# Splitting a ring of four PSUM banks into two and two in an eight-stage model kernel

## The chip, the cores and the metric

The kernel runs on one core of a Trainium2 chip. The metric is the device time of one execution in microseconds (us), from the first to the last instruction with what the device adds around them. Lower is better.

The engines are named as in the profile: PE is TensorE (PEld its weight loads), DVE is VectorE, ACT is ScalarE, POOL is GpSimd, SP is SyncE, whose queue issues most transfers. PSUM, where PE writes, has eight banks of 2 KB per partition here; one bank is a tile of 128 x 512 float32.

## The reference, cut to what matters

Four layers, each of a sequence part and a feed-forward part with a residual and a norm after each, on four sequences of 1024 tokens with 128 features. Only the last three parts run while the change is at work: the feed-forward part of layer 2 (pairs of a token and one of its two experts), the recurrence of layer 3 and its experts.

```python
def _L3_attn_ref(resid, ...):
    x = resid * lax.rsqrt(jnp.mean(resid * resid, -1, keepdims=True) + EPS) * norm_w
    skip = x @ skip_w.T
    xe = x @ in_w.T
    ...
    xs = jax.nn.silu(xc.transpose(0, 2, 1))
    delta = jax.nn.softplus(xs @ wd1.T @ wd2.T + wd2_b)
    A = -jnp.exp(A_log)
    Bm = xs @ wb.T
    Cm = xs @ wc.T
    def step(h, inp):
        d_l, b_l, c_l, x_l = inp
        h = jnp.exp(d_l[:, :, None] * A) * h + (d_l * x_l)[:, :, None] * b_l[:, None, :]
        y_l = jnp.einsum('ben,bn->be', h, c_l)
        return (h, y_l)
    _, ys = lax.scan(step, h0, (...))
    y = ys.transpose(1, 0, 2) + xs * W_D
    y = (y * jax.nn.silu(skip)) @ out_w.T
    return resid + y

def _L3_ffn_ref(x, Wr, br, W1, b1, W2, b2):
    probs = jax.nn.softmax(x @ Wr + br, axis=-1)
    ...
    gate = probs * keep
    h = jax.nn.relu(jnp.einsum('bth,ehf->betf', x, W1) + b1[None, :, None, :])
    y = jnp.einsum('betf,efh->beth', h, W2) + b2[None, :, None, :]
    return jnp.einsum('bte,beth->bth', gate, y)
```

Left out are a convolution of four taps along the tokens, which gives `xc`, and the choice of the most probable of eight experts up to a sum of 0.8, which gives `keep`. The scan runs over the tokens, with 256 channels of 16 states. All eight experts are computed for every token, and weighted by `gate`, which is zero where an expert isn't kept.

## The kernel before

The first 1350 us or so (layers 0 to 2) have PSUM pools of their own, which the change leaves alone. Then `l3_pools` (L1676) opens the pools of the last stage. `banks(...)` (L88) makes one pool per tag with so many banks each, and `psb` (L113) opens a tile of one bank under a tag. Before the change eight banks go to four tags: `y0` and `y1` with one bank each for the sums over the states, `da` with two for the decay, and `ff` with four for everything else.

`l3` (L1595) walks over eight halves: four sequences, two halves of 512 tokens. For each half `l3_scan` (L1816) does 16 steps, one per state. A step loads two rows (`bn`, `cn`) through SP's queue, multiplies on POOL (`db`, L1846), takes an exponential on ACT (`da`, L1850, into a `da` bank), scans along the tokens on DVE (L1851), multiplies on POOL again (`hc`, L1862), and PE adds `hc` into the `y0` and `y1` banks (`pys`); from the second sequence on, every second `hc` is first added to the one before it by a transfer that POOL issues (L1867). `hc` has four buffers, so POOL waits when PE is late with `pys`.

Between these steps the program lays other work in small pieces, in this order: the end of the half before (`l3_sum`, `l3_finish`: output projection `po`, norm, router `prl`, gates `gt`), the preparation of the next half (`l3_prepare`: `pt`, `pxe`, `pdb`, then the two `pd` tiles, which stay open together from their matmul through a chain on ACT and DVE until `ud` and `dl` are written, L1810 and L1811), what is left of a dispatch, the pairs of layer 2 (`l2_ffn`: `pt`, a `ph` of 128-column pieces with the weights `wx`, a `py`; its `l2_combine` opens `py0` and a norm tile), and three or four pieces of the last experts. Two gates per half (`psk`, L1894) go into `ff` as well.

The last experts (`l3_experts`, L1639) take the finished halves in order, a block of eight experts per half. One expert (`l3_ffn`, L1959) is four `ph` tiles of 128 x 512, each turned into `hh` by a Relu on ACT (L1977), then one `py` tile of 16 products (32 matmul records), which DVE adds to `h_acc` in four pieces with the gate as factor (L1993). Before a block, `l3_ffn_head` opens `pgt` and `pb2`; after it comes the last norm (a `pmv` tile, L155) and the output. Weights come as 512 KB transfers on SP's queue (`wh`, three buffers). A block may begin once its half's gates are there and four steps old. When the last half's end is through and the block under way is finished, all these pools are closed and one pool of eight `ff` banks takes their place for the last block (L1656 to L1658).

What sets the order: each engine runs its own queue in order. The program is written as above, but the framework (`TileContext` with `schedule_with_timeline_sim=True`) makes the order of each engine when the kernel is compiled: of the instructions whose inputs and buffers it believes ready it issues the one that stands first in the program. An instruction that opens a tile is ready only when a buffer of its tag has been given back by the last reader. So the size of a pool decides how far the engines run ahead and in which order, and at run time the same order is kept with semaphores for the waits. In the part that is concerned no order is written out by hand.

Of the kernel before, what the change touches and what calls it, by code (L numbers as in the profile page):

```python
# [58 lines left out]
class Net:  # L59
# [1579 lines left out]
    def l3_experts(self, fp):  # L1639


        c3 = self.c3
        heads, self.wh = [], {}

        def others():

            while len(heads) < 2 and c3["todo"] and ("all" in c3 or c3["todo"][0]["age"] > 3):
                heads.append((c3["todo"].pop(0), []))
            return heads[1:]

        i = 0
        while True:
            others()
            if "all" in c3 and c3["banks"]:

                c3["banks"].close()  # L1656
                c3["banks"] = None
                c3["ctx"].enter_context(self.banks(ff=8))  # L1658
            if heads:
                u = heads[0]  # L1660
                if not u[1]:
                    yield from self.l3_ffn_head(*u, fp)
                yield from self.l3_ffn(*u, i, fp, others)
                heads.pop(0)
                i += NE
            elif "all" in c3:
                return
            else:
                yield
# [6 lines left out]
    def l3_pools(self, ctx):  # L1676
        tc = self.tc
        sp = ctx.enter_context(tc.tile_pool(name="ssm", bufs=1))
        wp = ctx.enter_context(tc.tile_pool(name="ssm2", bufs=2))
        banks = ctx.enter_context(self.banks(y0=1, y1=1, da=2, ff=4))  # L1680
        self.mtags = dict(t="ff", h=("ff",), o="ff")
        self.c3.update(sp=sp, wp=wp, ctx=ctx, banks=banks)

# [257 lines left out]
    def l3_ffn_head(self, u, head, wp):  # L1941

        nc, c3, h = self.nc, self.c3, u["h"]
        ff = lambda s, n: self.psb("ff", s, n)
        acc = wp.tile([P, 4, D], F32, name="h_acc")
        head.append(acc)
        pg = ff([NE, 4, P], "pgt")
        for c in range(4):
            self.tr(pg[:, c, :], u["gt"][:, c, :])
        gT = wp.tile([NE, 4, P], F32, name="gT", bufs=1)  # L1950
        nc.scalar.copy(gT, pg)
        yield
        pb = ff([P, 4, D], "pb2")
        for c in range(4):
            self.mm(pb[:, c, :], gT[:, c, :], c3["b2"])
        nc.vector.tensor_add(acc, pb, self.xN[u["b"]][:, 4 * h : 4 * h + 4, :])
        yield

    def l3_ffn(self, u, head, i0, wp, others):  # L1959

        nc, c3, b, h, gt, acc = self.nc, self.c3, u["b"], u["h"], u["gt"], head[0]
        ff = lambda s, n: self.psb("ff", s, n)
        NK = F3 // P
        x = self.xT[b][:, h * 512 : h * 512 + 512]
        ahead = None
        for e in range(NE):
            if i0 + e == 0:
                for k in range(2):
                    self.l3_weights(k, wp)
            self.l3_weights(i0 + e + 2, wp)  # L1970
            w = self.wh.pop(i0 + e)
            hs = []
            for k in range(NK):
                ph = ff([P, 512], "ph")
                self.mm(ph, w[:, k * P : (k + 1) * P], x)
                ht = wp.tile([P, 512], F32, name="hh", bufs=6)
                nc.scalar.activation(ht, ph, AF.Relu, bias=self.col("h_b1", i=e * NK + k))  # L1977
                hs.append(ht)
                yield
            py = ff([P, 4, D], "py")  # L1980
            for c in range(4):
                for k in range(NK):
                    self.mm(
                        py[:, c, :],
                        hs[k][:, c * P : (c + 1) * P],
                        w[:, F3 + k * D : F3 + (k + 1) * D],
                        k == 0,
                        k == NK - 1,
                    )
                if c == 1:  # L1990
                    yield
            for c in range(4):
                nc.vector.scalar_tensor_tensor(  # L1993
                    acc[:, c, :],
                    py[:, c, :],
                    gt[:, c, e : e + 1],
                    acc[:, c, :],
                    ALU.mult,
                    ALU.add,
                )  # L2000
            yield

            if e >= NE - 3:
                if ahead is None and others():
                    ahead = self.l3_ffn_head(*others()[0], wp)
                if ahead is not None:
                    next(ahead, None)
        for f in ahead or ():
            pass
        self.norm(wp, acc, b, 4 * h, 4, last=True, ps=ff, act=True)  # L2010

# [193 lines left out]
```

## Time and profile before

| what | us |
|---|---|
| median of 3 runs | 2294.14 (2287.42 to 2300.56) |
| the profiled execution | 2289.61 |
| its span, first to last instruction | 2287.8 |
| PE busy over the span | 1974.5 (86%) |
| POOL busy over the span | 1023.3 (45%) |
| first product of the first half on POOL (`db`, L1846) | 1386.3 |
| first tile of the last experts (`pgt`) | 1541.3 |
| last product of the last half on POOL (`hc`, L1862) | about 2150 |
| last matmul of the last experts | 2279.3 |

The profile is of one execution. Its page cuts the span into 40 slices of 57 us; the digit of an engine is its busy share in tenths, PEclk the clock that TensorE was granted, in tenths of full speed:

```profile
PE   6667979879999999999989876589888989898998
DVE  7457743424355565665555556686777787877521
ACT  6543443332244444444555456476767786767443
POOL 5100230000023235224243429988789979888500
PEclk9757989979999999999999987799999999999999
```

The change concerns the slices from the 25th on. In the views of groups a line holds the kernel's line, engine, operation, the tiles written and read, the shape, the count, then the busy time and the mean ns of one, and after the bar the idle time of the engine just before them and what ended it. A float32 product shows as two matmul records.

### The profile page before, as it was taken

To read this page: it belongs to the slowest core of one execution; us is meant where nothing else is said; L and a number is where in the kernel's file an instruction comes from. 1 tells how busy PE (TensorE), PEld (TensorE's weight loads), DVE (VectorE), ACT (ScalarE), POOL (GpSimd) and SP (SyncE) were. 2 spreads that over 40 slices of the span, in tenths; PEclk is the share of its full clock that TensorE was granted. 3 is DMA by queue.
4 is the path that set the end of the run, shared out by engine and by line. 5 is a ranking of instruction groups with operands and counts; after the bars stand their busy time and mean duration, and the time that the engine had idled before them with its cause. 6 is when DMAs were issued, how large, how long until landed. Compare 5 with 4: busy or idle time off the path is not lost.

```text
span 2287.8 us, 46393 instructions
## 1 busy us (share of the span) xinstructions
PE 1974.5 (86%) x17806; PEld 1382.2 (60%) x17806; DVE 1351.7 (59%) x3693; ACT 1207.2 (53%) x2621; POOL 1023.3 (45%) x812
## 2 busy tenths in 40 slices
PE   6667979879999999999989876589888989898998
PEld 3455655444477777787767664346555656565666
DVE  7457743424355565665555556686777787877521
ACT  6543443332244444444555456476767786767443
POOL 5100230000023235224243429988789979888500
PEclk9757989979999999999999987799999999999999
DMA  3000110005000010031223147456776666676421
GB/s 107 0 15 23 30 39 1 19 10 174 1 3 2 3 35 15 17 91 46 76 70 88 32 142 231 127 182 196 202 204 178 177 169 192 175 208 178 122 60 51
DMA packets 138558, 211.10 MB, mean 92 GB/s; under 512 B 18597, under 2 KB 75936, under 8 KB 137952
## 3 DMA queue, kind: packets, MB, share of 16 engines
q1 hardware_dynamic: 126192, 173.87, 24.7%
q0 software_dynamic: 12144, 34.26, 7.1%
q8 instruction: 140, 2.29, 0.4%
q14 instruction: 82, 0.67, 0.1%
HBM read 160.29 MB, written 23.16 MB: 80 GB/s over the span
## 4 chain that ended last, share of the span: by engine, by line
PE 40%; DVE 13%; ACT 11%; issue 4%; DMA 2%; POOL 1%; SPq 0%; ACTq 0%; DVEq 0%; POOLq 0%
PE py L127 7%; PE ph L127 6%; PE po L1126 5%; DVE db L1851 5%; PE pqk L127 4%; PE pa_m L127 4%; PE kp_mo L127 3%; PE pr L1196 2%; PE pv L127 2%; PE pys L127 2%; ACT hh L1977 2%; ACT da L1850 1%; PE pt L131 1%; PE kp_mo L131 1%; ACT xN L174 1%
## 5 line engine op out<-in xcount | busy, mean ns | idle before, releaser
L1059 POOL TENSOR_TENSOR qt<-r_q,sb_c_turn 128x256 f32<-128x256 f32 (+1 forms) x256 | 164.0, 661 | 448.5 <-ACT r_q L1051 442.9
L1862 POOL TENSOR_TENSOR hc<-db,cn 128x1024 f32<-128x1024 f32 x128 | 312.9, 2463 | 63.5 <-PE pys L127 27.1
L127 PEld LDWEIGHTS py<-wh,hh 128*128 128x128 f32 x2048 | 248.6, 193 | 85.6 <-issue 36.1
L1846 POOL TENSOR_TENSOR db<-ud,bn 128x1024 f32<-128x1024 f32 x112 | 284.1, 2593 | 12.7 <-DMA wh<-in_wH 6.2
L127 PE MATMUL py<-wh,hh 128*128 128x128 f32 x2048 | 257.1, 278 | 22.9 <-ACT hh L1977 12.5
L127 PE MATMUL ph<-xT,wh 128*128 128x512 f32 x512 | 250.3, 606 | 16.8 <-ACT hh L1977 5.9
L1977 ACT ACTIVATE hh<-ph,sb_cols 128x512 f32<-128x512 f32 x256 | 170.6, 681 | 131.9 <-PE ph L127 105.5
L1117 DVE TENSOR_TENSOR a<-pa_m,sb_c_near 128x256 f32<-128x256 f32 x256 | 96.7, 420 | 202.6 <-PE pa_m L127 202.6
L1074 ACT ACTIVATE kN<-kp_mo,sb_c_trig 128x128 f32<-128x128 f32 x448 | 130.2, 372 | 132.0 <-PE kp_mo L131 122.2
L1850 ACT ACTIVATE da<-dl,aneg 128x512 f32<-128x512 f32 x224 | 153.1, 689 | 77.8 <-DVE db L1851 76.6
L127 PE MATMUL pys<-hc,sb_c_ident 128*128 128x512 f32 x324 | 159.7, 621 | 29.3 <-POOL hc L1862 21.3
L1851 DVE TENSOR_TENSOR_SCAN db<-da,carry,db 128x512 f32<-128x512 f32 x128 | 158.0, 1268 | 21.1 <-POOL db L1846 11.9
L1851 DVE TENSOR_TENSOR_SCAN db<-da,db 128x512 f32<-128x512 f32 x128 | 149.6, 1207 | 9.5 <-POOL db L1846 6.0
L127 PEld LDWEIGHTS ph<-xT,wh 128*128 128x128 f32 x512 | 89.8, 194 | 98.1 <-issue 57.1
L1993 DVE SCALAR_TENSOR_TENSOR h_acc<-py,gt,h_acc 128x128 f32<-128x128 f32 x256 | 71.8, 343 | 124.6 <-PE py L127 124.0
L127 PE MATMUL pqk<-xT,wE 128*128 128x256 f32 x512 | 136.8, 390 | 8.2 <-ACT coT L1193 4.2
L127 PEld LDWEIGHTS pys<-hc,sb_c_ident 128*128 128x128 f32 x324 | 61.0, 199 | 96.7 <-issue 60.6
L729 POOL DMA_INDIRECT orows<-o,ix x20 | 18.9, 944 | 186.6 <-DVE o L727 160.4
L127 PEld LDWEIGHTS pqk<-xT,wE 128*128 128x128 f32 x512 | 89.0, 194 | 22.0 <-DVE cv L1036 8.1
L131 PE MATMUL pt<-sb_c_ident,xN 128*128 128x128 f32 x224 | 54.4, 343 | 51.4 <-ACT xN L174 32.2
L1193 ACT COPY coT<-pt 128x512 f32<-128x512 f32 x64 | 37.6, 587 | 116.1 <-PE pt L131 116.1
L127 PE MATMUL po<-ht,wD 128*128 128x512 f32 x192 | 94.3, 598 | 0.0
(456 smaller groups left out, 4340.2 us busy)
## 6 DMA issues: line engine op xcount, KB each, us to landing
wx<-in_wF SPq DMA_DIRECT2D x92, 384.0 KB, 3.3
bn<-rows SPq DMA_DIRECT2D x128, 256.0 KB, 5.0
cn<-rows SPq DMA_DIRECT2D x128, 256.0 KB, 4.3
wh<-in_wH SPq DMA_DIRECT2D x64, 512.0 KB, 4.1
hc<-hc POOLq DMA_DIRECT2D x47, 512.0 KB, 6.6
xrows<-zero SPq DMA_DIRECT2D x4, 1472.0 KB, 11.9
xg<-xrows SPq DMA_DIRECT2D x20, 256.0 KB, 3.0
yrows<-ys SPq DMA_DIRECT2D x20, 256.0 KB, 3.3
```

Of the source, the lines that this page charges most:

```text
L127: return self.nc.tensor.matmul(out=out, lhsT=lhsT, rhs=rhs, start=start, stop=stop)
L131: self.nc.tensor.transpose(out, in_, self.ident[0:n, 0:n])
L1059: nc.gpsimd.tensor_mul(u["qt"][:, m, a:], u["q"][:, a:], c2["turn"][:, m, o + a : o + 2 * P])
L1074: self.nc.scalar.activation(u["kN"][:, c, m, :], pk[:, c, :], AF.Copy, scale=trig[:, k, m : m + 1])
L1117: nc.vector.tensor_mul(u["a"][:, i, :, :], pa[i], self.c2["near"][:, None, :].to_broadcast([P, 2, P]),)
L1126: self.nc.tensor.matmul(out=u["po"][self.HALF[j], i, c, :], lhsT=lhsT, rhs=rhs, start=key not in u["begun"], stop=True, skip_group_check=True,
L1846: nc.gpsimd.tensor_mul(db, ud, bc[0])
L1850: nc.scalar.activation(da, dl[:, ec, :], AF.Exp, scale=aneg[:, j : j + 1])
L1851: nc.vector.tensor_tensor_scan(db[:, ec, :], da, db[:, ec, :], carry[:, ec, n : n + 1] if h else 0.0, ALU.mult, ALU.add,)
L1862: nc.gpsimd.tensor_mul(hc, db, bc[1])
L1977: nc.scalar.activation(ht, ph, AF.Relu, bias=self.col("h_b1", i=e * NK + k))
L1993: nc.vector.scalar_tensor_tensor(acc[:, c, :], py[:, c, :], gt[:, c, e : e + 1], acc[:, c, :], ALU.mult, ALU.add,)
```

## The change

The four banks `ff` of the last stage become two tags of two banks each: `ff` and `ex`. The last experts' tiles (`pgt`, `pb2`, `ph`, `py`) now open under `ex`; the preparation, the ends of the halves, the router, the gates, the norms (the last one too) and the pairs of layer 2 stay under `ff`. For the last block, the one pool of eight becomes `ff` with two and `ex` with six. No instruction is added or removed, and no tile changes its size.

```diff
@@ l3_experts @@
                 c3["banks"].close()
                 c3["banks"] = None
-                c3["ctx"].enter_context(self.banks(ff=8))
+                c3["ctx"].enter_context(self.banks(ff=2, ex=6))
@@ l3_pools @@
-        banks = ctx.enter_context(self.banks(y0=1, y1=1, da=2, ff=4))
+        banks = ctx.enter_context(self.banks(y0=1, y1=1, da=2, ff=2, ex=2))
         self.mtags = dict(t="ff", h=("ff",), o="ff")
@@ l3_ffn_head @@
-        ff = lambda s, n: self.psb("ff", s, n)
+        ff = lambda s, n: self.psb("ex", s, n)
@@ l3_ffn @@
-        ff = lambda s, n: self.psb("ff", s, n)
+        ff = lambda s, n: self.psb("ex", s, n)
...
-        self.norm(wp, acc, b, 4 * h, 4, last=True, ps=ff, act=True)
+        self.norm(wp, acc, b, 4 * h, 4, last=True, ps=self.bank("ff"), act=True)
```

## The prediction, made before the change was run

> **What bounds the kernel now.** I read the page's row of slices first, then the busy time by stretches, then the groups on TensorE, and last the timeline of the experts alone. The change touches only what runs after about 1372 us, when the recurrence has its own PSUM pools.
>
> Busy time of each engine by stretch. The columns are the stretch, its length, busy us of PE, PEld, DVE, ACT and POOL with instruction counts, the granted clock, the DMA share and GB/s:
>
> ```profile
> 1372.00:1456.00 84.00, 54.46 (x200) 33.36 (x199) 54.02 (x93) 51.12 (x112) 78.12 (x47) 0.78 0.64 201
> 1456.00:1541.00 85.00, 61.00 (x247) 37.24 (x248) 70.36 (x114) 50.65 (x100) 79.45 (x35) 0.88 0.51 157
> 1541.00:1650.00 109.00, 97.69 (x513) 66.64 (x511) 74.59 (x154) 75.66 (x163) 87.72 (x50) 0.97 0.67 199
> 1750.00:1850.00 100.00, 90.48 (x430) 56.39 (x429) 77.42 (x163) 81.83 (x155) 91.08 (x49) 1.00 0.65 176
> 2050.00:2150.00 100.00, 93.21 (x464) 60.90 (x463) 72.34 (x137) 66.94 (x103) 85.82 (x43) 1.00 0.67 182
> 2150.00:2221.00 71.00, 65.14 (x368) 46.60 (x366) 22.60 (x78) 31.88 (x52) 0.00 (x0) 1.00 0.22 65
> 2221.00:2288.00 67.00, 58.18 (x320) 41.54 (x320) 10.79 (x42) 24.64 (x41) 0.00 (x0) 0.93 0.16 48
> ```
>
> Three stages. Until 1541 POOL is the bound (158 of 169 us busy) and PE has slack (115 of 169). From 1541, where the last experts begin, to 2150 PE and POOL are both near 90%. After 2150 only experts are left and PE runs nearly alone. PE's work is fixed, and experts left over at 2150 run in the end stage, so from 1541 on the end is PE's work plus PE's idle time. In 1541 to 2150 PE is busy 550 of 609 us. These 59 us are what the change can shrink or stretch. Their causes stand in the groups on PE from 1541 to 2150 (busy, mean ns, then idle time before them and who ended it):
>
> ```profile
> L127 PE MATMUL py<-wh,hh 128*128 128x128 f32 x1536 | 194.4, 278 | 21.7 <-ACT hh L1977 11.8 <-ACT ys L1510 5.1 <-ACT db L1785 2.2
> L127 PE MATMUL ph<-xT,wh 128*128 128x512 f32 x391 | 192.5, 605 | 13.2 <-ACT hh L1977 5.9 <-ACT ys L1510 3.4 <-DVE h_acc L1993 2.2
> L127 PE MATMUL pys<-hc,sb_c_ident 128*128 128x512 f32 x204 | 98.5, 605 | 7.8 <-DMA hc<-hc 7.8
> L127 PE MATMUL ph<-xgT,wx 128*128 128x128 f32 x153 | 21.4, 282 | 4.9 <-ACT ys L1510 1.5 <-ACT dl L1811 1.4 <-ACT ln_sd L164 1.1
> L127 PE MATMUL psk<-xnT,sb_s_in 128*128 128x512 f32 x24 | 12.6, 608 | 3.7 <-ACT hh L1977 3.7
> ```
>
> Experts (`wh`) wait for ACT to release pairs' and preparation's banks (`ys`, `db`), and a gate (`psk`) waits for an expert's bank. This is how a full shared ring looks.
>
> **How many banks each side needs.** For every PSUM tile I took the time from its first matmul to the end of its last reader, pairing matmuls and readers in order. From 1541 to 2150 the experts hold 0, 1, 2, 3, 4 banks for 46, 274, 215, 69 and 6 us (1.5 on average); the others hold 1.2. All four are held for 156 of 609 us. Mean holds: expert `ph` 2.8 us, expert `py` 7.5, pair `ph` 5.0, pair `py` 2.2, `pd` 16.2 (two at once), `prl` 12.1, `pxe` 10.2. From 1372 to 1541, without experts, the others hold three banks for 44 us and four for 43 us.
>
> **Part by part.** No instruction is added, removed or resized, and no DMA; only which tile may open when. The order on each engine is made anew at compile time, so holds are the safest currency.
>
> (a) *Removed: waits across the two groups.* From the rows above: `py` on `ys` 5.1 and on `db` 2.2, `ph` on `ys` 3.4, `psk` on `hh` 3.7: **-14 us** at most; 0 if something else is late at the same place. I take all of it.
>
> (b) *Added in the end stage up to 2221.* The seventh block of experts still runs on the small ring, now of two. How one expert goes there today:
>
> ```profile
> 2204.58 0.19 PEld L127 LDWEIGHTS py<-wh,hh 128*128 128x128 f32 x1 [0.24 <-issue]
> 2205.01 0.61 PE L127 MATMUL py<-wh,hh 128*128 128x128 f32 x4
> 2205.21 0.69 ACT L1977 ACTIVATE hh<-ph,sb_cols 128x512 f32<-128x512 f32 x1 [0.17 <-PE ph L127]
> ...
> 2206.96 1.02 PE L127 MATMUL ph<-xT,wh 128*128 128x512 f32 x2
> 2207.82 3.06 PE L127 MATMUL py<-wh,hh 128*128 128x128 f32 x26
> 2208.08 0.69 ACT L1977 ACTIVATE hh<-ph,sb_cols 128x512 f32<-128x512 f32 x1 [2.18 <-PE ph L127]
> 2210.72 2.74 PE L127 MATMUL ph<-xT,wh 128*128 128x512 f32 x6
> 2210.92 1.13 DVE L1993 SCALAR_TENSOR_TENSOR h_acc<-py,gt,h_acc 128x128 f32<-128x128 f32 x4 [3.49 <-PE py L127]
> ```
>
> After its first six `py` matmuls PE slips in the next expert's first `ph`, while ACT makes the fourth `hh`. That needs three banks: `py`, the fourth `ph`, the next `ph`. With two, the slipped `ph` comes after `py`: the fourth `hh` (0.1 + 0.69 us) is covered by six matmuls of 0.11 only, about 0.2 us idle. The second `ph` then waits for `py`'s bank (1.13 us on DVE and 0.1 of signals) behind one `ph` of 0.86: 0.4 idle. So 0.6 us an expert, with 8 experts: **+5 us**. Nothing can hide it: no other PE work is left. Bounds 3 and 10. After 2221 the new split gives the experts six banks; there they hold four at most, so nothing; the 3.7 us at the switch of pools stays (bounds -4 and 0).
>
> (c) *Added from 1541 to 2150.* I took the experts' tiles in order and asked whether the tile two places before still held its bank at the start: 101 of 256 times, 125 us in all. Carried forward (a delayed tile delays what follows, and the next lateness counts only beyond it) this makes 100 us. That is the upper bound: nothing else fills a gap. The lower is 0: some 150 us of other PE work (550 less the experts' 387 and 13 of their heads) could lie in all gaps. The nearest row for how many stay open is `py`'s wait for the last relu, a gap that every expert has today:
>
> ```profile
> PE py L127 <- ACT hh L1977: 12.4, 15, 1.8
> POOL hc L1862 <- PE pys L127: 27.1, 11, 9.1
> ```
>
> 15 of 48 experts, 31%. So 0.31 x 100 = **+31 us**. Behind a waiting `ph` in PE's queue stand the state sums (`pys`), preparation and pairs; for `pys` POOL already waits 27.1 us (second row), so a longer stall there stops the recurrence too.
>
> (d) *Added from 1372 to 1541.* Held beyond two banks: 44 x 1 + 43 x 2 = 130 bank-us. One pair tile takes 5.0 + 2.2 = 7.2, so at most 18 pair tiles of 1.8 us PE work (21.4 us over 19 tiles, 13.6 over 22, and the transposes) go past 1541, where PE is full: 32 us. If the two banks were never free, the total held, 366 of 338 bank-us, puts off 4 tiles: 7 us; and if they fill gaps of (c), 0. The holds are mostly queueing and shrink when fewer tiles are open: **+8 us**. POOL and scan do not use these banks; what covers a late preparation is the margin before its half's first product: `pd` is released at 1440 and 1541, POOL starts at 1472 and 1559. Later halves have none (1664.6 against 1667.6, 1878.5 against 1878.0), but experts have work for some 20 us there: a block starts 11 to 32 us after its gates. I take 0.
>
> Sum: -14 + 5 + 31 + 8 = **+30 us**. The profiled execution took 2289.6 us (span 2287.8 and 1.8 around it): 2320. It lies 4.5 below the median of the runs, 2294.1, so **2324 us**.
>
> **A rule of the skill against a row.** From 1372 the granted clock follows PE's load in the stretches above: 0.78 at 65% busy, 0.88 at 72%, 0.97 to 1.00 at 88 to 93%. Falling from 90% to 86% between the last two points would cost 0.02 of 550 us, 12 us; as 88% and 93% both stay near full clock I leave it out of the sum and keep it for the upper end. The Trainium skill (TensorE: Matmul & The Clock Gate, "A second HAM failure mode: psum-queue depth-cycling") says that micro-idles from cycling through PSUM banks can make the clock oscillate. By it the sum would be 2336 instead of 2324. The same page (section "HAM oscillation") reports a kernel in which PSUM double-buffering changed the time by only 1%. That speaks for no change here.
>
> **Rivals.** *Faster:* (a) happens and other work fills the experts' gaps. Place: PE between 1541 and 2150. Price: -14 and +5, 2285, or 2280 if the end stage is filled too. For it: some 150 us of other PE work against 100 us of gaps, and an order remade for two banks. Against: a full pool of four at 156 of 609 us loses by being cut, and today a third of the analogous gaps stays open. It decides if under a tenth of the 100 us stays open. *No change:* the experts hold at most two banks for 534 of 609 us, so the limit hardly binds: 2294, with (a) and (c) cancelling. *Much slower:* preparation with `pd` holding both banks for 16 us, while `prl` (12 us) needs one, loses about 10 us per half in five halves that have no margin, 50 us, of which the experts' 20 us of stock covers part: 2324 + 30 = 2354. Against: from 1750 the others hold three banks for only 21 of 400 us. *Not as it says:* the buffers are counted per tag, so the split is certain; if both groups kept their order the price is (c)'s.
>
> **How the numbers follow.** Forecast 0.58, faster 0.20, no change 0.12, much slower 0.10. Own range of the forecast: (c) between 15 and 60, (d) 0 to 20, 2300 to 2365. The range that should hold 8 of 10 takes in the faster rival: low 2277, high 2368 (2294 - 14 + 10 + 60 + 6 and the 12 of the clock). About 0.5% (11 us) is what a measurement tells from no change. Below 2283: 0.20; within: 0.13; above 2305: 0.67.
>
> **What would show it.** (a) right: no expert `ph` or `py` ended by `ys` or `db`, `psk` not by `hh`. (b): in the end stage 32 `py` matmuls in one go with a gap of about 0.4 us before the second `ph`, ended by `h_acc`. (c): expert `ph` idle from 13 to about 40 us, ended by `hh` and `h_acc`; PE's idle time from 59 to some 85 us. (d): pairs' last tiles after 1730 instead of 1718. It is wrong if PE's idle time stays at 60, or if POOL is seen waiting for `ud` or `dl` by over 5 us in most halves, or if the clock falls below 0.95 after 1541.

## The result and the profile after

The changed kernel takes 2364.3 us (median of 4 runs, 2355.3 to 2372.2) against 2290.8 us of the kernel before, measured beside it: 1.0316 times as long, 95% interval 1.0285 to 1.0347, or 74 us. A second measurement gave 1.0315 (1.0280 to 1.0351). The forecast of 2324 us had the direction, and its range of 2277 to 2368 us holds the result, near the upper end; the 30 us of its sum are less than half of what came. The profiled execution has a span of 2370.4 us, 82.6 more than the one before, and is the slowest of its four.

The slices of the page, as they were shown of the kernel before:

```profile
PE   6667978979999999999889756788898889999888
POOL 5000320000123243233333178988488878989100
PEclk9757979979999999999999878899898999999999
```

POOL's row now has a 4 among the eights and nines: within the recurrence it stops for a good part of one slice. PE's clock falls to 8 tenths in places where it stood at 9. Busy time by stretches again, now cut at the first product of a half (the second half starts at 1488, the third at 1577, the fourth at 1719; columns as in the prediction, some rows left out):

```profile
1488.00:1577.00 89.00, 68.09 (x243) 39.89 (x244) 68.19 (x106) 47.97 (x89) 76.49 (x34) 0.87 0.46 143
1577.00:1719.00 142.00, 120.87 (x615) 83.06 (x614) 90.32 (x184) 90.60 (x188) 97.46 (x57) 0.92 0.67 185
1719.00:1828.00 109.00, 95.61 (x484) 65.69 (x484) 80.22 (x163) 81.69 (x150) 95.03 (x54) 0.94 0.65 178
...
1922.00:2017.00 95.00, 84.88 (x377) 53.51 (x376) 75.01 (x138) 67.79 (x114) 81.49 (x41) 0.95 0.66 177
...
2208.00:2300.00 92.00, 84.41 (x435) 55.32 (x433) 23.92 (x82) 36.95 (x56) 0.54 (x1) 0.98 0.19 55
2300.00:2370.00 70.00, 58.25 (x320) 41.49 (x320) 13.61 (x56) 25.38 (x42) 0.00 (x0) 0.94 0.18 53
```

One half stands out: the third takes 142 us where it took 109 (1559.0 to 1667.6). The four halves after it take 109, 94, 95 and 99 us against 113, 98, 90 and 98, and the last 93 against 84. The groups on POOL in that half say why:

```profile
L1846 POOL TENSOR_TENSOR db<-ud,bn 128x1024 f32<-128x1024 f32 x17 | 42.3, 2537 | 36.6 <-ACT dl L1811 35.0 <-DVE ud L1810 1.5
L1862 POOL TENSOR_TENSOR hc<-db,cn 128x1024 f32<-128x1024 f32 x16 | 38.7, 2611 | 4.9 <-PE ph L127 3.2 <-ACT xgT L1470 1.2 <-PE pys L127 0.5
```

POOL waits 35.0 us, once, for `dl`: the preparation of the fourth half is late. The last product of the recurrence comes at 2208.5 instead of 2149.6.

On PE, from the experts' first tile (1558) to that product, the groups that were shown before:

```profile
L127 PE MATMUL py<-wh,hh 128*128 128x128 f32 x1497 | 198.7, 289 | 16.2 <-ACT hh L1977 14.8
L127 PE MATMUL ph<-xT,wh 128*128 128x512 f32 x376 | 198.0, 631 | 30.6 <-ACT hh L1977 24.9 <-DVE h_acc L1993 5.6
L127 PE MATMUL pys<-hc,sb_c_ident 128*128 128x512 f32 x204 | 98.0, 603 | 0.0
L127 PE MATMUL ph<-xgT,wx 128*128 128x128 f32 x184 | 27.5, 297 | 7.7 <-DMA wx<-in_wF 4.0 <-issue 2.7 <-ACT db L1785 0.8
L127 PE MATMUL psk<-xnT,sb_s_in 128*128 128x512 f32 x26 | 14.6, 643 | 0.8 <-ACT dl L1811 0.8
```

The waits across the groups are gone: nothing of the experts is ended by `ys` or `db`, and `psk` no longer by `hh` (3.7 before). In their place the experts' `ph` waits 24.9 us for `hh` and 5.6 for `h_acc`, for its own group's two banks. And this is one expert of the end stage, alone on PE:

```profile
2256.85 1.02 PE L127 MATMUL ph<-xT,wh 128*128 128x512 f32 x2
...
2257.05 1.13 DVE L1993 SCALAR_TENSOR_TENSOR h_acc<-py,gt,h_acc 128x128 f32<-128x128 f32 x4 [6.51 <-PE py L127]
2257.97 0.69 ACT L1977 ACTIVATE hh<-ph,sb_cols 128x512 f32<-128x512 f32 x1 [4.18 <-PE ph L127]
2258.23 0.30 PEld L127 LDWEIGHTS ph<-xT,wh 128*128 128x128 f32 x2 [1.19 <-DVE h_acc L1993]
2258.23 3.09 PE L127 MATMUL ph<-xT,wh 128*128 128x512 f32 x6 [0.36 <-DVE h_acc L1993]
...
2260.19 0.30 PEld L127 LDWEIGHTS ph<-xT,wh 128*128 128x128 f32 x2 [0.81 <-ACT hh L1977]
2260.99 0.80 PEld L127 LDWEIGHTS py<-wh,hh 128*128 128x128 f32 x6 [0.50 <-ACT hh L1977]
2261.16 4.11 PE L127 MATMUL py<-wh,hh 128*128 128x128 f32 x32
2261.36 0.69 ACT L1977 ACTIVATE hh<-ph,sb_cols 128x512 f32<-128x512 f32 x1 [0.42 <-PE ph L127]
2262.09 2.98 PEld L127 LDWEIGHTS py<-wh,hh 128*128 128x128 f32 x26 [0.30 <-ACT hh L1977]
...
2265.10 1.02 PE L127 MATMUL ph<-xT,wh 128*128 128x512 f32 x2
```

From one first `ph` to the next it takes 8.25 us. In the kernel before the end of one `py` follows the other by 7.01 us when nothing else comes between. The 32 `py` matmuls run in one piece with no `ph` of the next expert inside, and the waits for a bank stand on the weight loads too (PEld, 1.19 before the second `ph`, 0.81 before the fourth, 0.50 before `py`), which here aren't done ahead of the matmul. The last wait, 0.30 us, is of another kind: the fourth `hh` is itself the weights of the next `py` matmuls.

The account of the two profiled executions: the end is the last product plus the experts that are left. Before, 2149.6 + 16 experts of 8.11 us each; after, 2208.5 + 18 of 8.52 (other work between them included). So 58.9 us are a later recurrence, 2 x 8.52 = 17 two more experts left over, and 16 x 0.41 = 7 their slower pace. That makes 83. Of the 58.9 us, 33 are the third half, 9 the last, and 7 the first; 9 stand before the first product (1394.9 against 1386.3). These last 9 aren't all the change's: the kernel without the switch, in an experiment below, has the banks of the kernel before at that time, and its first product came at 1391.6.

### The profile page after: what moved, and what is told of

Read it like the earlier page. It is cut to its first block, busy times and chain, and to the rows that moved or that the text cites. A ratio compares the mean times of both kernels' runs of the same rounds, so it can differ in the third digit from the quotient of the medians.

```text
span 2370.4 us, 46344 instructions
## 1 busy us (share of the span) xinstructions
PE 2026.5 (85%) x17806; PEld 1406.9 (59%) x17806; DVE 1356.2 (57%) x3693; ACT 1211.7 (51%) x2621; POOL 1024.9 (43%) x812
## 4 chain that ended last, share of the span: by engine, by line
PE 42%; DVE 14%; ACT 12%; issue 3%; POOL 1%; DMA 1%; SPq 0%; ACTq 0%; DVEq 0%; POOLq 0%
PE py L127 8%; PE ph L127 7%; PE po L1126 5%; PE pqk L127 4%; PE pa_m L127 4%; DVE db L1851 4%; PE kp_mo L127 3%; PE pys L127 2%; PE pv L127 2%; PE pr L1196 2%; ACT hh L1977 2%; ACT da L1850 2%; PE pt L131 1%; PE kp_mo L131 1%; DVE h_acc L1993 1%
## 5 line engine op out<-in xcount | busy, mean ns | idle before, releaser
L127 PE MATMUL ph<-xT,wh 128*128 128x512 f32 x512 | 267.7, 630 | 36.5 <-ACT hh L1977 24.9
L127 PEld LDWEIGHTS py<-wh,hh 128*128 128x128 f32 x2048 | 257.0, 200 | 70.0 <-ACT hh L1977 45.0
L127 PE MATMUL py<-wh,hh 128*128 128x128 f32 x2048 | 267.7, 286 | 18.1 <-ACT hh L1977 16.1
```

The source lines that it names most:

```text
L127: return self.nc.tensor.matmul(out=out, lhsT=lhsT, rhs=rhs, start=start, stop=stop)
```

## The experiments

Chips differ (the kernel before took 2291, 2329, 2294 and 2293 us in the four sets of runs), so each kernel is compared with runs of the kernel before on its own chip, and a total that was expected in us is read as a ratio to 2291. The first four kernels ran where the kernel before takes 2329.

**Is it the early pairs?** The pairs use the idle `ex` banks until the third half begins:

```diff
-        self.mtags = dict(t="ff", h=("ff",), o="ff")
+        self.mtags = dict(t="ex", h=("ex",), o="ex")
...
             nxt = iter(())
+            if i == 2:
+                self.mtags = dict(t="ff", h=("ff",), o="ff")
```

> The changed kernel, but the pairs of layer 2 open their tiles under ex until the third half's scan begins (ex has no user until then), and under ff after it. Theory 1 (pairs starve preparation, gates and ends on the two ff banks, so the halves start late: +9, +16, +18, +51 us): the fourth half starts within 20 us of the kernel before (1668), no 35 us gap on POOL, total 2305 to 2325. Theory 2 (the experts' ring of two makes PE idle and lowers its clock): only the 18 us lost before the third half come back at most, total 2345 to 2365.

Measured: 1.0302 (1.0283 to 1.0320). The third half took 125 us instead of 142, so half of that stall went; the total did not follow, and 1.0302 of 2291 us, 2360, is what theory 2 had. But the experiment doesn't separate the theories: the first half took 111 us instead of 93, so that from its first to its last product the recurrence took 811 us, against 814 in the changed kernel and 763 before. 46 experts were done at the last product, as in the changed kernel, and each of the rest took 8.6 us.

**One side at a time.** With one bank for the decay instead of two there is a fifth bank to give away. The control has five shared; then the experts alone are held to two, then the rest alone (the first edit is to the kernel before, the other two to the changed one):

```diff
-        banks = ctx.enter_context(self.banks(y0=1, y1=1, da=2, ff=4))
+        banks = ctx.enter_context(self.banks(y0=1, y1=1, da=1, ff=5))
```

```diff
-        banks = ctx.enter_context(self.banks(y0=1, y1=1, da=2, ff=2, ex=2))
+        banks = ctx.enter_context(self.banks(y0=1, y1=1, da=1, ff=3, ex=2))
```

```diff
-        banks = ctx.enter_context(self.banks(y0=1, y1=1, da=2, ff=2, ex=2))
+        banks = ctx.enter_context(self.banks(y0=1, y1=1, da=1, ff=2, ex=3))
```

> The kernel before with one bank for the decay (da) instead of two and five shared ff banks. A control for the next two; both theories: 2285 to 2330, by what one decay bank costs the scan.

> The changed kernel with one da bank and three ff banks, experts still on two. Theory 1: the early halves start as in the control and the total is within 15 us of it. Theory 2: 45 us or more above the control.

> The changed kernel with one da bank and three banks for the experts, ff still two. Theory 1: 45 us or more above the control, with the fourth half's scan late by 40 us. Theory 2: within 20 us of the control.

| kernel | ratio to before | interval | third half, us | last product | experts left | us each |
|---|---|---|---|---|---|---|
| control, 5 shared | 1.0075 | 1.0050 to 1.0099 | 110.9 | 2204.4 | 16 | 7.94 |
| 3 and 2 for the experts | 1.0311 | 1.0294 to 1.0329 | 118.9 | 2222.9 | 19 | 8.60 |
| 2 and 3 for the experts | 1.0262 | 1.0237 to 1.0287 | 144.4 | 2262.1 | 15 | 7.74 |

The control stays near the kernel before, as expected. Both others cost: 57 us (medians 2401.6 against 2344.5) for the experts' two banks, 46 (2390.2) for the others' two. The control on POOL's groups (1500 to 2200) and on PE shows where each has its loss. First POOL's `db` with three `ff` banks, then with two:

```profile
L1846 POOL TENSOR_TENSOR db<-ud,bn 128x1024 f32<-128x1024 f32 x110 | 281.0, 2555 | 0.0
```

```profile
L1846 POOL TENSOR_TENSOR db<-ud,bn 128x1024 f32<-128x1024 f32 x103 | 264.2, 2605 | 44.1 <-ACT dl L1811 34.9 <-DVE ud L1810 8.3 <-POOL db L1846 0.9
```

With three `ff` banks POOL never waits for a preparation; with two it waits 44.1 us, 34.9 of them for `dl`, the same stall as in the changed kernel. On PE, the experts' `ph` during the recurrence, with five shared and with two of their own:

```profile
L127 PE MATMUL ph<-xT,wh 128*128 128x512 f32 x390 | 198.0, 615 | 12.6 <-DVE h_acc L1993 2.4 <-ACT hh L1977 2.0 <-ACT db L1785 1.9
```

```profile
L127 PE MATMUL ph<-xT,wh 128*128 128x512 f32 x368 | 195.3, 635 | 37.5 <-ACT hh L1977 24.8 <-DVE h_acc L1993 7.3 <-issue 5.2
```

2.0 us of waiting for `hh` become 24.8, as in the changed kernel, and 368 of the 512 records are done by the last product instead of 390. So there are two losses and neither theory is right by itself. Apart they add to 103 us; together, in the changed kernel with its two decay banks, they cost 74. That the experts catch up while the recurrence stands still would explain this, and the last row of the table fits it (the recurrence ends 58 us later than in the control, with one expert fewer left), but no run shows it by itself. Nor does any run hold the order and change the banks alone: each kernel has an order of its own, made when it is compiled, so these costs are of waiting and of the new order together.

**The third bank of an expert.** In the changed kernel `py` opens under `ff`, all the time in one kernel, and only for the experts issued after the last scan in the other:

```diff
-            py = ff([P, 4, D], "py")
+            py = self.psb("ff", [P, 4, D], "py")
```

```diff
-            py = ff([P, 4, D], "py")
+            py = self.psb("ff" if "all" in c3 and c3["banks"] else "ex", [P, 4, D], "py")
```

> The changed kernel, but the experts' py tiles open under ff, so that ex holds only ph, pgt and pb2. If the experts' ring of two is the limit (8.25 us an expert alone in the changed kernel against 7.01 before, 56 experts outside the last block, so 69 us): the next expert's first ph is back inside py, an expert alone takes 7.0 to 7.3 us and the ratio to before is 1.010 to 1.020. If the two ff banks limit the preparation and the ends, these get worse by the py holds, the halves start later than in the changed kernel and the ratio is 1.030 to 1.050.

> The changed kernel, but py opens under ff for the experts that the program issues after the last scan, until the pools are switched (about 6 experts). Both theories: the scans as in the changed kernel; an expert alone takes 7.0 to 7.3 us there instead of 8.25, so 6 to 9 us less than the changed kernel: ratio to before 1.027 to 1.030.

The first took 1.0355 (1.0328 to 1.0382). 48 experts are done at the last product, as before the change, but that product comes 25 us later than in the changed kernel: the third and the fourth half take 143 and 139 us, and POOL's `db` waits 56.7 us for preparations. This is the second branch of what was expected. The second took 1.0291 (1.0264 to 1.0317), which overlaps the changed kernel's interval. In its trace the last three experts before the last block end 6.77, 8.53 and 7.85 us apart, against 8.26, 8.99 and 9.12 in the changed kernel. That is near the kernel before (7.44, 8.29 and 6.53), though not the 7.0 to 7.3 expected. Only three experts were issued that late, not six, so some 3 us is all there was to win, which the intervals can't tell from nothing.

**Cut in two, or one bank fewer.** The kernel before with three banks in the shared ring, the fourth left unused:

```diff
-        banks = ctx.enter_context(self.banks(y0=1, y1=1, da=2, ff=4))
+        banks = ctx.enter_context(self.banks(y0=1, y1=1, da=2, ff=3))
```

> The kernel before with three shared banks instead of four, one bank left unused. If it is the cutting that costs (idle banks on one side while the other waits): less than the changed kernel though it has one bank fewer, ratio 1.010 to 1.025. If it is only the number of banks that each tile can reach: 1.030 or more.

1.0427 (1.0398 to 1.0455): slower than the cut ring, so the second branch of what was expected holds. Cutting costs less than losing one of the four banks.

**Whose backlog makes the preparation late?** In the changed kernel all tiles of the pairs go to `ex`, the combine stays in `ff`; beside it, on the same chip, the changed kernel once more:

```diff
-        self.mtags = dict(t="ff", h=("ff",), o="ff")
+        self.mtags = dict(t="ex", h=("ex",), o="ex")
```

> The changed kernel with all tiles of the pairs under ex (their combine stays under ff), so that ff has only preparation, ends, gates, routers and norms. If the backlog of pairs on two banks makes the fourth half late: its scan follows the third's within 120 us (142 in the changed kernel, 109 before), and the total is still 1.02 or more above before, because the experts now share two banks with the pairs until about 1760. If it is preparation and ends among themselves (two pd tiles at once, the router): 135 us or more between these scans as in the changed kernel.

> The changed kernel once more, beside the one with the pairs on ex on the same chip: ratio to before 1.028 to 1.035, 135 to 145 us from the third half's first product to the fourth's, 8.2 to 8.3 us an expert alone before the last block.

With the pairs away the third half takes 108.8 us, the changed kernel again 143.7 (and 8.25 us an expert alone). POOL's `db` (1500 to 2200) of the kernel with the pairs on `ex`:

```profile
L1846 POOL TENSOR_TENSOR db<-ud,bn 128x1024 f32<-128x1024 f32 x108 | 273.8, 2611 | 5.0 <-issue 2.6 <-DVE ud L1810 2.4
```

No wait for `dl` is left. So it is the pairs in `ff` that make the fourth half late, not preparation and ends among themselves. Counting tiles: when the third half begins, 31 of the 47 pairs' `ph` have been opened in the kernel before, 24 in the changed one, 29 here. The first tile of the fourth half's preparation opens 29, 73 and 26 us after that. The total is 1.0386 (1.0352 to 1.0421), for the experts now share two banks with the pairs: 43 are done at the last product, which comes 19 us earlier than in the changed kernel beside it. The half after, the fourth, took 135 us. Its trace shows the pairs again, by another way: POOL also issues the gathers (`yg`, L1529) that fetch the pairs' results for the combine, and in that half these stood 15.9 us idle, 4.2 of them for the results to be written and 7.4 for a norm (`xN`), against 4.6 us in the kernel before. What the rest of the 135 us is was not tried.

**A version that is a little better than both.** The profile of the kernel before has a wait at the switch to eight banks, which the prediction had left standing. The kernel before without the switch:

```diff
-            if "all" in c3 and c3["banks"]:
-
-                c3["banks"].close()
-                c3["banks"] = None
-                c3["ctx"].enter_context(self.banks(ff=8))
```

> The kernel before without the switch to eight banks for the last block. The last block holds four banks at most, so the ring of four should do, and the 3.7 us wait at the switch and the slow 1.9 us after it go: ratio 0.9970 to 0.9990. If the last block needs more than four: 1.000 or above.

0.9981 (0.9965 to 0.9998), 4 us less, with an interval that ends just below 1. On PE at that place, first the kernel before, then without the switch:

```profile
2221.07 5.30 PE L127 MATMUL ph<-xT,wh 128*128 128x512 f32 x8 [3.67 <-DVE ln_nm L168]
```

```profile
2215.45 4.11 PE L127 MATMUL py<-wh,hh 128*128 128x128 f32 x32
2219.40 3.60 PE L127 MATMUL ph<-xT,wh 128*128 128x512 f32 x8
```

The new pool made the first `ph` wait 3.67 us for the last tile of the old ones, and its eight records then took 5.30 us instead of 3.60. The clock shows why: after the wait it was granted at 0.50 from 2221 to 2224 us, and without the switch at 1.00 through the same eight records. Without it PE goes straight on, and the last block's eight experts take 57.9 us instead of 61.9. Four shared banks are enough for it.

## Why the prediction was right or wrong

The direction and the first mechanism hold: the experts on two banks make PE wait. The size doesn't, and the step that failed most is (d): a late preparation was priced at nothing, and the two `ff` banks, which make it late, cost 46 us when tried alone. That the measured time still lies inside the range is in part luck: (d) lies outside its bounds of 0 to 20, (c) at or near the top of its 15 to 60, and the two losses came to less together than apart.

(a) *Waits across the groups go:* right in the rows, 14 us of them are gone. But the PE time isn't seen to be won: waits for the own group's banks take their place, and PE's idle time from the experts' first tile to the last product rises from 59 to 72 us. The forecast had some 85, and "PE's work is fixed": PE's busy time there rose too, by 28 us, which the sum had at nothing.

(b) *End stage, 0.6 us an expert:* the mechanism was right, `py` in one piece and a wait for `h_acc` before the second `ph` (0.36 us where 0.4 was worked out). The size was not: 1.24 us an expert (8.25 less 7.01), 10 us for eight and so at the upper bound. The working counted when the bank is free and let the matmul follow at once. In the trace the weight load waits for the bank too, so such a wait also uncovers a load, and the fourth `ph` and `py` wait again (0.81 and 0.50 on PEld).

(c) *During the recurrence, +31:* with (b) and (a) this is what the experiment with two banks for the experts alone measures: 57 us against 36 - 14 = 22. With 10 us for (b) this leaves 47 us for (c) if nothing of (a) is won and 61 if all of it is, against the 31 of the sum, and the carried lateness of 100 us held as an upper bound. The share of 31% left open came from a wait that has a slipped `ph` to cover it, and that cover is what the change takes away; this is a likely reason, which no run tests alone.

(d) *The early stage, +8, with preparations covered by their margins:* this failed. The two-bank `ff` alone cost 46 us. The prediction saw that pairs would be put off, and counted only their PE work. What it missed is their place in the program: a pair that is late stands ahead of the next preparation, and takes the next free bank (so the program reads, and the counts of tiles fit it). So the backlog of seven pairs became a preparation 44 us later, and a margin of 18 us at the third half, none at the fourth, could not cover 35 us of POOL's waiting. That the experts would have work meanwhile did not make up for it: at the last product, 59 us later than before, two experts fewer were done. The prediction's own sign, POOL waiting for `ud` or `dl` by over 5 us in most halves, came in one half only.

*The rivals.* Faster and no change are out. "Much slower" gave 2354 us and so came nearest, with the wrong place: it had `pd` against the router in each of five halves. The halves from the fifth to the seventh took 94 to 99 us as before; one half stood still, the third, and for the pairs. "Not as it says" is out: no cross-group wait is left in the rows.

*The clock.* From the experts' start to the last product it fell from 0.98 to 0.94 on average, which was a sign that the prediction was wrong (below 0.95). In the traces the clock there is either full or half (1.0 or 0.5 of full speed): half in 5 stretches of together 20 us before, in 13 of together 77 us after. The row of the kernel before (0.97 at 88% busy) would not have told that, with PE still 89% busy; the Trainium skill's remark on short idle times from cycling through PSUM banks (TensorE: Matmul & The Clock Gate, "A second HAM failure mode: psum-queue depth-cycling") would fit this back and forth. That the banks cause it here no run shows: the longest stretches at half clock, 10 us each, begin at 1682 and 1706 us, where PE itself waits in the third half (busy 4.4 of the 10 us from 1680, 2.0 of the 5 us from 1700). Of the 28 us by which PE's busy time grew there (550 to 578), 550 x (0.983 / 0.941 - 1), about 25, would be the clock's. Whether this lengthened the run, or only filled time in which PE would have waited, no run here separates.

## What to carry to other kernels

Before cutting a shared ring, count for each side how many buffers its pipeline holds at once when it runs at full pace, not on average: an expert here needs three (the output, the last input being evicted, the next one being written), though it held at most two for 534 of 609 us. Work that falls behind in a greedy order moves ahead of everything issued later, so a shortage in one kind of work shows up as lateness of another, further down the program. And two shortages in one kernel need not add (103 us apart, 74 together): curing the one shows the other.

## What the runs showed of the hardware

Here a wait for a PSUM bank stands on the weight load as well: where the bank is late, PEld idles 0.50 to 1.19 us and the load of 0.2 to 0.3 us comes out from behind the matmul. PE's busy time hides this. Six `ph` records in a row, shown as 2.74 us with banks free, take 3.09 with the second `ph`'s load late. In the end stage, at a granted clock of 0.98, the experts' `ph` has a mean of 629 ns against 594 before the change at a clock of 1.00, and PE reads 84 of 92 us busy while each expert takes 1.24 us longer. In this trace the busy share of PE does not show how well it is fed; the spacing of equal work does.
